# Where the sums of k's exponentials are made in a linear-attention layer: within ScalarE's exponentials or by a VectorE reduction

## The chip, the cores and the metric

The kernel runs on one core of a Trainium2 chip. That core has five engines that work side by side and wait for each other by semaphores: TensorE (PE, matmuls; its weight loads are listed as PEld), VectorE (DVE), ScalarE (ACT), GpSimd (POOL) and SyncE (SP), which here issues the transfers. The metric is the device time of one execution in microseconds (us), and the time given is the median of several executions.

## The reference

An input x of 32 batches x 256 tokens x 256 features goes through four residual layers in a row. Layers 0 and 2 are Mamba layers (a selective scan over time with 512 channels and 16 states), layer 1 is softmax attention with 16 heads, and layer 3 is linear attention. All are modulated by a condition vector. The change lies in layer 3, which is, cut to what matters:

```python
xn = layernorm(x, norm_scale, norm_bias)
q, k, v = xn @ Wq + bq, xn @ Wk + bk, xn @ Wv + bv
k = where(mask, -inf, k);  v = where(mask, 0, v)        # then split into 16 heads
q = softmax(q, axis=-1)                                 # over a head's 16 features
k = softmax(k, axis=2)                                  # over the 256 tokens
attn = einsum('bhse,bhsd->bhed', k, v)
y = einsum('bhtd,bhed->bhte', q, attn)
h = layernorm(y) * (1 + scale) + shift                  # scale, shift from the condition
x = x + silu(h) @ film_out_W + film_out_b
```

The softmax of k runs over tokens. Each of the 256 features of k has its own maximum and its own sum of 256 exponentials.

## The kernel before

All arithmetic is fp32. A batch is worked on whole: 256 tokens x 256 features, as two groups of 128 partitions. A Mamba layer is split into a part ahead of the scan (`mamba_ahead`: norm, input projection, convolution, the steps `dt` and `dtu` that go out to memory and come back spread over the partitions as `dtr` and `dtur`) and the scan itself (`mamba_scan`). The scan has 16 steps, numbered k, each over 128 partitions x 1024 elements. Step k takes these operations:

- POOL makes `b`, the product of `dtur` and `B` (tile `b`, a ring of four buffers).
- ACT makes `h`, four exponentials of `dtr` (a ring of two PSUM buffers).
- DVE runs the recurrence over time, a scan, into `h` on even k and on odd k into `b`.
- The product with `C` is made by DVE on even k and by POOL on odd k (the last step of layer 2 counts as even).
- PE sums over states into `y`, which frees the `b` buffer. After every eighth step DVE multiplies `y` with a gate into `u`.

The scans of the layers 0 and 2 of different batches follow each other without a break: in the steady state a scan of layer 0 for one batch and a scan of layer 2 for the batch two before it take turns. Everything else (the parts ahead of the scans, attention and linear attention) is placed between the scan's steps on the same engines.

The order on every engine is not written by hand. The layers are Python generators that call `at(cost)` and then an engine. `at` opens a `Step` with a planned cost in us and a due time. `Plan.call` records the operation in the step, and `use` records which tiles it reads and writes. `Plan.order` then plays the steps forward with these costs and picks for each engine the step with the earliest due time among those that can begin soon. `carry_out` issues them all in that order, from one line, L468, so that nearly every instruction in the profile has that line. Several constants steer it. `SHIFT` holds one offset for the due time of each step of a layer, the same in every batch. `NEED` says how much work PE must have had lately for the plan to leave it alone. Where there is less, `usual` may put a filler matmul on PE, `y<-rows,zeros`, which adds zero to `y`. `LATE` and `NEAR_ACT` bear on which step ACT takes next when steps need different activation tables. `Exp`, `Silu` and `Softplus` are used with different tables, and a change of table is an instruction of its own on ACT (`ACT_TABLE_LOAD`).

In `linear_attention` k lies with features on partitions and tokens along the row, in PSUM. DVE takes the row maxima (`kmx`), POOL clamps and negates them, ACT makes the exponentials `ke` in two instructions of 128x256 with `kmx` as bias, DVE sums each row into `ks` and takes the reciprocal, and ACT multiplies `ke` by it. Then PE transposes `ke` (`tr_k`), and ACT copies the result to `kvt`, from which PE makes `kv`.

Of the kernel before, what the change touches and what calls it, by code (L numbers as in the profile page):

```python
# [8 lines left out]
F32 = mybir.dt.float32  # L9
I32 = mybir.dt.int32  # L10
AF = mybir.ActivationFunctionType
ALU = mybir.AluOpType
AX = mybir.AxisListType
# [3 lines left out]
P = 128  # L17
S = 256
D = 256
DC = D // P  # L20
# [36 lines left out]
for _n, _k in COLS:  # L57
# [20 lines left out]

SHIFT = {
    "0": (  # L80
        -33, -39, 49, 69, -13, -21, 58, -32, -13, -36, 7, -37, -50, -1, -44, -40, -43, -13, 18, -41, -36, -47,
        -80, -79, 24, -26, -5, -17, -9, 34, 75, -49, 27, 18, 56, 17, 69, 59, 79, 79, 74, 63, -22, 38, -56, -58,
        -50, -76, 3, 14, -1, 41, 23, 28, 53, 49, 6, 61, 34, 75, 75,
    ),
    "0s": (
        -8, -74, -45, -9, -61, -75, -1, 18, -58, 23, 27, -12, -1, -16, 19, 64, -41, -18, -5, 59, 23, 65, -13,
        20, 8, 65, -63, -5, 65, -77, 21, 57, 80, 76, 71, 79, 66, 53, 57, 74, 49, 72, 52, 46, 36, 25, -46, -3,
        -67, 6, 60, 26, -19, 29, 74, 64, 56, 18, 73, 13, 26, 22, 44, 17, -8, 73, 38, 40, 71, 77, 60, 57, 74, 51,
        40, -47, 6, 32, -43, 61, 52, 16, 53, -20, -75, -25, -43, 15, 27, -41, 46, -76, -9, -10, -47, -3, 33,
        -22, 42, -77, -43, -22, -10, -2, -29, 57, 17,  # L90
    ),
    "1": (
        -64, -4, -23, -21, 49, 48, -49, -43, -80, -32, -70, -18, 3, 3, -25, -46, -54, -70, -75, -1, -8, -30, 34,
        79, -14, -67, 8, -5, 14, -36, -52, -14, -7, -22, -60, 9, -59, -18, -64, 1, 1, 26, -16, 17, 46, -30, -15,
        32, 9, 30, -12, 10, -20, 42, -47, -14, 23, -22, -68, 27, 32, 19, 2, -1, -80, -62, -79, -54, -79, -47,
        -25, -15, -21, -10, 1, 21, -2, 31, -58, 2, -3, -49, 6, 78, -43, -6, -35, 11, 23, -14, -58, 40, 44, -1,
        -23, -50, 2, -35, -73, -69, -17, -5, -2, -79, -57, 27,
    ),
    "2": (
        -18, 34, 39, -51, -30, -27, 5, 75, -63, -79, -32, -5, -41, -36, 42, -64, -65, -11, -35, 3, -13, -46,  # L100
        -43, -42, -41, -54, -68, 20, -39, -29, -57, -67, -21, -5, -32, 54, 2, -58, 50, -60, 12, -44, -37, 5, 71,
        7, 64, -66, -80, -44, -71, -78, -63, -69, -78, -80, -79, -53, -5,
    ),
    "2s": (
        27, -39, 3, -15, 79, -10, 35, -22, 71, 45, -25, 54, -1, 32, -7, 37, 53, -22, 60, -60, 9, -12, -10, 6,
        -9, -23, -5, -37, 29, 26, 15, 11, 42, -10, 70, -30, -11, 26, 48, 26, -67, -61, -52, 27, -1, 57, -35,
        -14, -16, -33, 27, 39, 23, -38, 41, -5, 0, -3, 40, -60, 6, -49, -5, 43, 75, 47, 47, 59, 18, 50, 11, 65,
        42, 55, 24, 46, 47, 43, 52, 64, 64, 29, 5, -35, 2, -56, 30, -23, 43, -61, 5, -20, -47, -18, 40, -26,
        -80, -66, -78, 31, -53, 1, -35, -55, 7, 41,
    ),  # L110
    "3": (
        -5, 8, -23, -48, -53, -70, -75, -55, -50, -34, 7, -31, -45, -58, -61, -75, -43, -72, -18, -76, 6, 0,
        -79, -42, -57, 45, 9, 77, 33, -38, -7, -34, 44, -52, 12, 32, -55, -56, -69, 46, -68, -67, -79, -53,
    ),
    "w": (
        73, 75, 58, 71, 33, 47, 28, 57, 27, 50, 16, 34, 52, 42, -58, -10, -11, -12, -6, 9, 47, 25, 58, 59, 17,
        70, 19, 12, -23, 30, -51, -46, -77, -80, -32, -40, -10, 21, 69, 76, 72, 80, 72, 80, 72,
    ),
}

# [130 lines left out]
class Plan:  # L251
# [1 line left out]


    NEAR = 0.36
    NEED = 1.12
    IDLE = 0.47
    LATENCY = 0.15
    SWITCH = 1.3
    LATE = 0.04  # L260
    NEAR_ACT = 0.76

    def __init__(self, nc, tc):
        self.nc, self.tc = nc, tc
# [5 lines left out]
    def at(self, cost, then=0.0, ahead=0.0, area=None):  # L270
        self.kind[1] += 1
        shift = SHIFT.get(self.kind[0], ())
        n = self.kind[1]
        ahead -= 0.01 * shift[n] if n < len(shift) else 0.0
        self.step = Step(cost, self.due - ahead, then, 2140 * cost if area is None else area)
        self.step.kind = tuple(self.kind)
        self.step.number = len(self.steps)
        self.steps.append(self.step)
        return self.step

    def call(self, engine, name, args, kw):
        s = self.step
        assert s.engine in (None, engine)
        s.engine = engine
        s.calls.append((name, args, kw))
        if name == "activation":
            f = args[2]
            table = None if f in (AF.Identity, AF.Copy) else f
            assert s.table in (None, table) or table is None
            s.table = s.table or table  # L290
        out = kw.get("out", args[0] if args else None)
        for a in (*args, *kw.values()):
            if isinstance(a, View):
                self.use(s, a, a is out)

    def use(self, s, view, written):
        t = view.tile
# [15 lines left out]
    def order(self):  # L313
# [41 lines left out]
        def usual(found, t0):  # L355
# [4 lines left out]
            end = at + s.cost  # L360
            if clock.recent(end - clock.STRETCH, end) + s.area >= self.NEED * clock.ENOUGH:
                return one
# [7 lines left out]
        def best(e):  # L370
            found = []
            for s in can[e]:
# [5 lines left out]
                if e == "scalar" and s.table not in (None, table):  # L378
                    more, due = self.SWITCH, due + self.LATE
                found.append((begin + more, due, s.number, s, begin, more))  # L380
# [6 lines left out]
            if e == "scalar":  # L387
                near = self.NEAR_ACT
            return min((f for f in found if f[0] <= t0 + near), key=lambda f: (f[1], f[2]))
# [103 lines left out]
def kernel(ctx: ExitStack, tc: tile.TileContext, t, out: bass.AP):  # L493
    nc = tc.nc
# [174 lines left out]
    for L in (0, 2):  # L669
        Aneg[L] = ctile([P, IC, QB, SG], f"Aneg{L}")  # L670
        a = Aneg[L].rearrange("p c q g -> p (c q g)")
# [28 lines left out]
    nc = plan  # L700
    at = plan.at

    def space(name, bufs, **kw):
        return Space(ctx.enter_context(tc.tile_pool(name=name, bufs=bufs)), bufs, **kw)

    xp, w2, w1 = space("xp", 5), space("w2", 2), space("w1", 1)
    bcp, rep, ring, small = space("bcp", 5), space("rep", 2), space("ring", 4), space("small", 4)
# [110 lines left out]
    def transposed(src, nm):  # L818

        ps = mm(f"tr_{nm}")  # L820
        pv = ps.rearrange("p (c t) -> p c t", c=2)
        at(0.5, area=0.0)
        for c in range(2):
            for s in range(2):
                nc.tensor.transpose(pv[:, c, s * P : (s + 1) * P], src[:, s, c * P : (c + 1) * P], ident)
        return pv
# [213 lines left out]
    def by_token(xn, w, bias, nm):  # L1040

        ps = mm(nm)
        pv = ps.rearrange("p (s d) -> p s d", s=ST)
        for s in range(ST):
            at(0.96)
            for k in range(DC):
                nc.tensor.matmul(pv[:, s, :], lhsT=xn[:, k, s * P : (s + 1) * P], rhs=w[:, k, :],
                                 start=(s == 0 and k == 0), stop=False)
        at(0.9)
        nc.tensor.matmul(ps, lhsT=one_at(bias, P), rhs=row(bias), start=False, stop=True)  # L1050
        return pv
# [112 lines left out]
    def linear_attention(b):  # L1164
        nm = f"3_{b}"
# [6 lines left out]
        pv = ps.rearrange("p (c t) -> p c t", c=DC)  # L1172
# [6 lines left out]
        kmx = small.tile([P, DC], F32, name=f"kmx_{nm}", tag="kmx")  # L1179
# [2 lines left out]
        at(0.25)  # L1182
        nc.gpsimd.tensor_scalar(kmx, kmx, 0.1 * FAR, -1.0, ALU.max, ALU.mult)
        ke = w1.tile([P, DC, S], F32, name=f"ke_{nm}", tag="ke")
        at(0.9)
        for c in range(DC):
            nc.scalar.activation(ke[:, c, :], pv[:, c, :], AF.Exp, bias=kmx[:, c : c + 1])
        ks = small.tile([P, DC], F32, name=f"ks_{nm}", tag="ks")
        at(0.85)
        nc.vector.tensor_reduce(out=ks, in_=ke, axis=AX.X, op=ALU.add)  # L1190
        nc.vector.reciprocal(ks, ks)
        at(0.74)
        for c in range(DC):
# [1 line left out]
        pv = transposed(ke, f"k{nm}")  # L1195
# [6 lines left out]
        pv = by_token(xn, wt["L3_v"], "L3_v_b", f"v_{nm}")  # L1202
# [6 lines left out]
        pv = by_token(xn, wt["L3_q"], "L3_q_b", f"q_{nm}")  # L1209
# [15 lines left out]
        pv = transposed(q, f"q{nm}")  # L1225
# [7 lines left out]
        pv = ps[:, : DC * P].rearrange("p (c e) -> p c e", c=DC)  # L1233
# [9 lines left out]
        pv = ps.rearrange("p (s d) -> p s d", s=ST)  # L1243
# [71 lines left out]
    for begin, L, b in sorted(layers):  # L1315
        begin = max(begin, end)
        end = begin + (LINEAR[1] if L == 3 else max(0.5, min(ATTN, until[b] - begin)))
        ends[L, b] = end
        layer = (attention if L == 1 else linear_attention)(b)
        gens.append((f"{L}", placed(layer, begin, end, (L, b), (L - 1, b))))  # L1320
        if L == 1:
            until[b] = max(until[b], end)
# [105 lines left out]
```

## Time and profile before

| what | value |
|---|---|
| median of 3 executions | 4544.42 us (4538.73 to 4545.05) |
| the profiled execution, its own time | 4539.75 us |
| its span, first to last instruction | 4537.7 us |
| mean granted TensorE clock | 0.977 of full speed |
| busy PE / DVE / ACT / POOL | 4128.3 / 3828.3 / 3515.6 / 3963.5 us |
| matmuls and filler among them, busy | 279.8 us in 990 rows |
| activation table loads | 419 rows, 537.6 us |
| moved by DMA | 583.65 MB, mean 129 GB/s |

A group's row names the line, the engine, the operation and its tiles (written <- read), then the shape and the count; after the bar come the busy time in us, the mean of one in ns, and the idle time of the engine just before these instructions, with what ended that idle time. An fp32 matmul of the program shows as two MATMUL rows. A row of waits gives the total in us, the number of waits and the longest one. A table of stretches gives for each stretch of time the busy time of every engine.

### The profile page before, as it was taken

To read this page: it belongs to the slowest core of one execution; us is meant where nothing else is said; L and a number is where in the kernel's file an instruction comes from. 1 tells how busy PE (TensorE), PEld (TensorE's weight loads), DVE (VectorE), ACT (ScalarE), POOL (GpSimd) and SP (SyncE) were. 2 spreads that over 40 slices of the span, in tenths; PEclk is the share of its full clock that TensorE was granted. 3 is DMA by queue.
4 is the path that set the end of the run, shared out by engine and by line. 5 is a ranking of instruction groups with operands and counts; after the bars stand their busy time and mean duration, and the time that the engine had idled before them with its cause. 6 is when DMAs were issued, how large, how long until landed. Compare 5 with 4: busy or idle time off the path is not lost. (4 is left out here: it accounts for less than half of the span.)

```text
span 4537.7 us, 77776 instructions
## 1 busy us (share of the span) xinstructions
PE 4128.3 (91%) x27576; PEld 2613.8 (58%) x27576; DVE 3828.3 (84%) x3879; ACT 3515.6 (77%) x7373; POOL 3963.5 (87%) x2544
## 2 busy tenths in 40 slices
PE   5889999999999999999999999999999999999987
PEld 4565555556555555565555555555555555556554
DVE  2768889888889898888998888988888988888865
ACT  2657888788887787888788888888778878888764
POOL 1968999889999998999999999999889999989865
PEclk7999999999999999999999999999999999999999
DMA  7433544554444554444554444455444455444322
GB/s 204 117 97 106 140 124 131 144 146 118 132 128 119 144 147 120 129 133 121 146 148 134 125 136 120 127 149 142 122 127 128 119 153 143 133 122 129 103 77 63
DMA packets 309268, 583.65 MB, mean 129 GB/s; under 512 B 45840, under 2 KB 207216, under 8 KB 308880
## 3 DMA queue, kind: packets, MB, share of 16 engines
q1 hardware_dynamic: 308880, 578.69, 46.0%
q8 instruction: 218, 3.57, 0.3%
q14 instruction: 170, 1.39, 0.1%
HBM read 365.19 MB, written 77.73 MB: 98 GB/s over the span
## 5 line engine op out<-in xcount | busy, mean ns | idle before, releaser
L468 POOL TENSOR_TENSOR b<-dtur,B 128x1024 f32<-128x1024 f32 x1024 | 2396.0, 2361 | 202.0 <-PE y L468 163.4
L468 ACT ACTIVATE h<-dtr,Aneg 128x256 f32<-128x256 f32 x4096 | 1700.6, 466 | 339.9 <-DVE b L468 248.1
L468 DVE TENSOR_TENSOR_SCAN h<-h,b 128x1024 f32<-128x1024 f32 x544 | 1240.1, 2284 | 159.8 <-ACT h L468 111.5
L468 POOL TENSOR_TENSOR b<-b,C 128x1024 f32<-128x1024 f32 x480 | 1130.9, 2359 | 116.0 <-DVE b L468 110.1
L468 DVE TENSOR_TENSOR_SCAN b<-h,b 128x1024 f32<-128x1024 f32 x480 | 1094.0, 2279 | 82.0 <-POOL b L468 80.6
L468 PE MATMUL y<-b,sel 128*32 128x256 f32 x8192 | 627.5, 393 | 72.3 <-POOL b L468 39.9
L468 DVE TENSOR_TENSOR b<-h,C 128x1024 f32<-128x1024 f32 x544 | 659.9, 1217 | 11.3
L468 PE MATMUL in<-hT,w_L_in 128*128 128x256 f32 x2048 | 530.2, 401 | 66.4 <-DVE nm L468 46.3
L468 ACT ACT_TABLE_LOAD x419 | 537.6, 1283 | 31.3 <-DMA dtr<-dtd 17.8
L468 PEld LDWEIGHTS in<-hT,w_L_in 128*128 128x128 f32 x2048 | 379.4, 196 | 201.6 <-DVE nm L468 59.7
L468 PEld LDWEIGHTS y<-b,sel 128*32 128x32 f32 x8192 | 185.5, 109 | 374.3 <-issue 124.3
L468 ACT ACTIVATE ex<-s 128x512 f32<-128x512 f32 x512 | 277.2, 594 | 132.8 <-PE s L468 130.1
L468 DVE TENSOR_REDUCE nm<-s 128x2 f32<-128x512 f32 x512 | 327.6, 677 | 52.2 <-PE s L468 52.1
L468 PE MATMUL s<-k,q 32*128 32x256 f32 x2048 | 325.0, 403 | 4.6 <-DVE yg L468 1.6
L468 PE MATMUL s<-q,k 32*128 32x256 f32 x2048 | 295.6, 404 | 8.7 <-DVE nm L468 5.2
L468 PE MATMUL y<-rows,zeros 128*128 128x256 f32 x990 | 279.8, 403 | 0.0
L468 PE MATMUL cv<-xc,taps 128*32 128x256 f32 x2048 | 182.7, 424 | 105.8 <-DMA xc<-xpad 76.2
L468 PEld LDWEIGHTS s<-k,q 32*128 32x128 f32 x2048 | 197.1, 185 | 127.5 <-issue 54.7
L468 PEld LDWEIGHTS s<-q,k 32*128 32x128 f32 x2048 | 178.4, 186 | 126.0 <-issue 49.9
L468 PE MATMUL o<-w_L_out,u 128*128 128x256 f32 x1024 | 243.0, 387 | 8.1 <-DVE u L468 3.9
L468 PEld LDWEIGHTS o<-w_L_out,u 128*128 128x128 f32 x1024 | 189.2, 191 | 56.7 <-DVE u L468 13.1
L468 PEld LDWEIGHTS y<-rows,zeros 128*128 128x128 f32 x990 | 171.9, 192 | 82.5 <-issue 68.2
(480 smaller groups left out, 5581.3 us busy)
## 6 DMA issues: line engine op xcount, KB each, us to landing
dtur<-dtud SPq DMA_DIRECT2D x256, 512.0 KB, 5.3
dtr<-dtd SPq DMA_DIRECT2D x256, 512.0 KB, 6.9
xc<-xpad SPq DMA_DIRECT2D x256, 129.5 KB, 2.4
xc<-xpad SPq DMA_DIRECT2D x256, 129.4 KB, 2.7
xc<-xpad SPq DMA_DIRECT2D x256, 129.2 KB, 2.3
xc<-xpad SPq DMA_DIRECT2D x256, 129.1 KB, 2.4
C<-bc SPq DMA_DIRECT2D x256, 128.0 KB, 2.6
B<-bc SPq DMA_DIRECT2D x256, 128.0 KB, 2.7
```

The costliest lines, as they stand in the source:

```text
L468: made.append(getattr(engine, name)(*[real(a) for a in args], **{k: real(v) for k, v in kw.items()}))
```

## The change

The two exponentials of k get a second output, the row sums (`accum_out`), so that `ks` is written by ACT. The DVE reduction goes, and its reciprocal stays as a step of its own. The planned costs of the two steps change with that (1.1 and 0.15 us in place of 0.9 and 0.85). `Plan.call` now counts `accum_out` as written. The offsets of all steps in `SHIFT`, and the constants `NEED`, `LATE` and `NEAR_ACT`, have other values, so the order of the instructions differs on every engine. Of `SHIFT` only the first row of one entry is shown here; all seven entries are replaced.

```diff
 SHIFT = {
     "0": (
-        -33, -39, 49, 69, -13, -21, 58, -32, -13, -36, 7, -37, -50, -1, -44, -40, -43, -13, 18, -41, -36, -47,
+        -12, -21, 77, 78, 40, 60, 71, -26, -18, -11, -2, -73, -49, -47, -80, -80, -80, -80, -67, -55, -45, -38,
...
     NEAR = 0.36
-    NEED = 1.12
+    NEED = 1.13
     IDLE = 0.47
     LATENCY = 0.15
     SWITCH = 1.3
-    LATE = 0.04
-    NEAR_ACT = 0.76
+    LATE = 0.14
+    NEAR_ACT = 0.52
...
             if isinstance(a, View):
-                self.use(s, a, a is out)
+                self.use(s, a, a is out or a is kw.get("accum_out"))
...
         ke = w1.tile([P, DC, S], F32, name=f"ke_{nm}", tag="ke")
-        at(0.9)
+        ks = small.tile([P, DC], F32, name=f"ks_{nm}", tag="ks")
+        at(1.1)
         for c in range(DC):
-            nc.scalar.activation(ke[:, c, :], pv[:, c, :], AF.Exp, bias=kmx[:, c : c + 1])
-        ks = small.tile([P, DC], F32, name=f"ks_{nm}", tag="ks")
-        at(0.85)
-        nc.vector.tensor_reduce(out=ks, in_=ke, axis=AX.X, op=ALU.add)
+            nc.scalar.activation(ke[:, c, :], pv[:, c, :], AF.Exp, bias=kmx[:, c : c + 1], accum_out=ks[:, c : c + 1])
+        at(0.15)
         nc.vector.reciprocal(ks, ks)
         at(0.74)
         for c in range(DC):
```

## The prediction

> **What bounds the kernel now.** The page first: no engine is at its peak, three are near it.
>
> ```profile
> PE 4128.3 (91%) x27576; PEld 2613.8 (58%) x27576; DVE 3828.3 (84%) x3879; ACT 3515.6 (77%) x7373; POOL 3963.5 (87%) x2544
> ...
> L468 POOL TENSOR_TENSOR b<-dtur,B 128x1024 f32<-128x1024 f32 x1024 | 2396.0, 2361 | 202.0 <-PE y L468 163.4
> ```
>
> Start and end dilute these shares, so I read the busy time of the steady stretch next, then POOL's waits in it.
>
> ```profile
> 400.00:4100.00 3700.00, 3427.36 (x23204) 2154.14 (x23204) 3251.87 (x3261) 3001.89 (x6299) 3387.02 (x2163) 0.99 0.48 132
> ```
>
> ```profile
> POOL b L468 <- PE y L468: 103.2, 89, 2.9
> POOL b L468 <- DVE b L468: 75.5, 77, 3.7
> POOL dtu L468 <- ACT dt L468: 14.0, 25, 0.7
> POOL b L468 <- DMA dtur<-dtud: 10.0, 4, 2.9
> ```
>
> The columns of the stretch are PE, weight loads, DVE, ACT, POOL: 93, 58, 88, 81 and 92%. DVE's row for the permuted residual (x<-x,og) comes at 2115.47 and, seven batches on, at 3051.11 us: 133.7 us a batch. POOL's own work in a batch, from its groups, is 32 x 2.36 (products with B) + 15 x 2.36 (with C) + 2 x 2.35 (dtu) + 1.27 + 4 x 1.34 (norm statistics) + 0.66 = 122.9 us. Its waits between 600 and 4000 us sum to 218 us, over 25.4 batches 8.6 each; 2 us are small gaps. So POOL paces the kernel, and the time follows POOL's waits: for PE's y (a ring buffer comes free) and DVE's scan. The change takes nothing from POOL.
>
> Last the edited operations.
>
> ```profile
> L468 ACT ACT_TABLE_LOAD x419 | 537.6, 1283 | 31.3 <-DMA dtr<-dtd 17.8 <-DVE b L468 3.4 <-PE dt L468 1.6
> ...
> L468 PE MATMUL y<-rows,zeros 128*128 128x256 f32 x990 | 279.8, 403 | 0.0
> ...
> L468 ACT ACTIVATE ke<-ke,ks 128x256 f32<-128x256 f32 x64 | 29.0, 500 | 20.0 <-DVE ks L468 20.0
> ...
> L468 ACT ACTIVATE ke<-k,kmx 128x256 f32<-128x256 f32 x64 | 26.8, 470 | 57.0 <-POOL kmx L468 57.0
> ...
> L468 DVE TENSOR_REDUCE ks<-ke 128x2 f32<-128x512 f32 x32 | 21.2, 662 | 2.4 <-ACT ke L468 2.4
> ...
> L468 DVE RECIPROCAL ks<-ks 128x2 f32<-128x2 f32 x32 | 5.3, 166 | 1.1
> ```
>
> All of the removed work is 21.2 us of DVE, 0.47% of the time.
>
> **The change part by part.** The instruction lists of both builds give counts: DVE 32 fewer, POOL and SP the same (2857 transfers), ACT 53 more, all table loads (421 to 474), PE 237 more, all filler matmuls (495 to 732). The rest is order.
>
> *The reduction goes:* 32 x 0.662 = 21.2 us of DVE. At most all of it returns, if DVE paced everywhere; nothing, where POOL does. DVE idles 12% of the steady stretch, so I credit a third: -7 us.
>
> *The accumulation:* 64 exponentials also write a sum. The trace has no such instruction. Below: 0, or less if it shortened the row, which an added output gives no reason for. Above: one more short ACT instruction each, nearest the shortest ACT row, the copy of xd at 0.36 us: 23 us. I take 0.2 (small DVE and POOL rows of two columns are 0.17 to 0.23): 13 us of ACT. ACT idles 25 us a batch in the steady stretch ((3700 - 3002)/27.7), which hides 0.4; uncovered, it costs those 13.
>
> *A new wait.* Before, v's scaling and an h step stand between exponentials and the multiply by 1/ks, and ACT waits 0.69 us (20.0/29). After, the multiply follows at once. On DVE the reciprocal now stands behind scan 6 (2.28) and its product (1.22). From the end of DVE's kmx: POOL 0.23 and hops, exponentials and sums 1.2, ACT ready at 1.6; reciprocal done at 3.7. ACT waits 2.1, 1.4 more (46 us in all). Behind it stands h 8 (1.67), done 2.6 after the reciprocal; DVE first has x (0.69), scan 7, a reduction and a subtraction, 4.3 us. Cover enough: 0. Transposes of ke follow it on PE; kv, which needs them, is three scan steps from where DVE uses it.
>
> *Table loads:* steady batches go from 13 to 15; dt's second half now stands apart from its first in the L0 scan, with a switch each way. The timeline of ACT shows what a switch costs:
>
> ```profile
> 2243.60 1.67 ACT L468 ACTIVATE h<-dtr,Aneg 128x256 f32<-128x256 f32 x4 [0.48 <-DVE b L468]
> 2245.29 1.28 ACT L468 ACT_TABLE_LOAD   x1
> 2246.59 0.60 ACT L468 ACTIVATE sz<-in 128x512 f32<-128x512 f32 x1
> ```
>
> 0.02 us lie on either side, so 1.30 each: 53 x 1.30 = 69 us of ACT. The Trainium skill (ScalarE: Activation LUTs, section What ACT_TABLE_LOAD costs) speaks harder against the change: 1.28 plus 1.38 of drain, 2.66 us a switch, which makes 141 us. The row decides: no drain is seen. 2.2 us a batch fit in the idle 25; I take 0, and 69 if each stands before an h that DVE awaits.
>
> *Fillers:* one is two rows, 279.8/495 = 0.57 us; 237 make 134 us, 4.2 a batch. PE has 9.8 idle ((3700 - 3427)/27.7). A filler takes the place of idle time or delays a real matmul. Ends: 0 and 134. I take 0, since the steady clock is 0.99 and PE waits for others, and keep 134 as a rival.
>
> *The order, the largest term.* I follow it from the end of the last L2 scan that POOL finishes (step 13), t = 0, in rows: scan 2.28, product 1.22, POOL 2.36. DVE: scan 14, product, to 3.5; scan 15 needs POOL's b 15, now behind C 13, at 4.8, and ends 7.1, its product 8.3. L0's scan 0 ends 10.6; two score reductions, newly first, 12.0; product 13.2, u 13.9, scan 1 16.2. POOL has done b 0 to 3 by 14.2 and waits 2.0 for it. Then its x needs yg (22.1 on DVE): 1.2 more. C 3 needs scan 3, behind two more reductions, 25.8: 2.3 more. So 5.5 in this place; before, the two batches from 2163 us waited 0.73 and 1.91 there. In return POOL's b 0 no longer waits: six long POOL operations now stand between dtu and it (before: four), 4.7 us more for dtu's store and dtur's load, which on SP keep their places behind the store of out; it waited 2.24 and 2.85. The old waits of 2.18 or 0.47 at b 8, 0.55 and 0.63 in L2 go as well, DVE being early there. New: C 13 1.0, C 11 0.9, hops of 0.1 to 0.3 about 1.0; kept: dtu and the memsets 0.9. Sum after 9.3, against 8.6: +0.7 x 28 steady batches = +20 us; with the spread of that walk (2 us a batch) -56 to +60.
>
> The start-up is reordered on SP too (the second x and some weights change places), where POOL waits for first data until 95 us; I take 0, +-5.
>
> *Sum:* -7 + 0 + 0 + 0 + 0 + 20 = +13, and +7 for the wait for the reciprocal and the sums where their cover fails one time in eight ((46 + 13)/8): +20. The profiled execution took 4539.75 us (span 4537.7), 4.7 under the median of 4544.4; against the median that is 4564.
>
> **The rivals.**
> *Faster:* the walk overrates the C 1 and C 3 waits, since DVE's rows overlap, and the end of the b 0, b 8 and L2 waits stays. At 7.7 a batch against 8.6: -25, 4519. At half of those two waits, 6.6 against 8.6: -56, 4488. For: the b 0 wait is 10 us by transfers alone in the view. Against: three reductions and yg now precede scan 3.
> *PE becomes the pacemaker (clearly slower):* fillers do not fill idle time but precede score matmuls. 123.9 + 4.2 busy + 9.8 idle is 137.9 a batch, +4.2 x 28 = +118: 4662. It decides if PE's unfilled idle stays above 5.6 a batch. For: PE is 93% busy. Against: the plan places a filler only where PE's next matmul would start late or leave PE too idle, and most of PE's waits in the steady stretch name DVE or a transfer.
> *Table loads on the path:* +69, 4613. For: DVE waits 71.7 us for h already. Against: ACT's own waits for DVE are 168.9.
> *No change:* reduction and reorder cancel, 4544.
> That the sums stay on DVE is excluded by its list.
>
> **How the numbers follow.** A measurement can tell about 0.2% (9 us). Likeliest: the small loss, 0.36 (4554 to 4600 on its own). Loads or PE on the path 0.13. No change 0.09. The small gain 0.27, the large 0.15. So faster 0.42, same 0.09, slower 0.49. The range leaves out the top of the PE case and the tail of the large gain: 4478 to 4645.
>
> **What would show it.** Right: POOL's waits for DVE b above 3.0 us a batch (now 75.5/25.4), those for PE y below 4; no more than a few us for dtur; ACT's wait for ks near 2 us; loads of 1.28 us. Wrong: a batch below 133.4 us (the gain), PE's idle unchanged beside 732 fillers (PE case), DVE's wait for h well above 71.7 (loads).

## The result, and the profile after

The changed kernel is slower: 4697.5 us (median of 4 executions, 4685.9 to 4708.4) against 4541.7 us. The ratio is 1.0332, with a 95% interval of 1.0313 to 1.0351. The direction was forecast, though by little more than a coin toss (0.49 against 0.42); the size was not: +156 us came where +20 stood, outside the range. The profiled execution has a span of 4684.2 us, at a mean granted clock of 0.975. Nearly all of the loss is there at nearly the same clock: that span is 146 us longer than the one before, which had 0.977. The other three executions, at 0.966 to 0.969, take 11 to 23 us more.

The page after, in its row of engines, and the stretch from 400 to 4100 us (columns as before: PE, weight loads, DVE, ACT, POOL, then PEclk, DMA share, GB/s):

```profile
PE 4234.1 (90%) x28050; PEld 2713.5 (58%) x28050; DVE 3834.8 (82%) x3847; ACT 3591.1 (77%) x7490; POOL 3970.8 (85%) x2544
```

```profile
400.00:4100.00 3700.00, 3397.31 (x22843) 2168.98 (x22844) 3144.79 (x3119) 2965.96 (x6179) 3269.92 (x2083) 0.98 0.46 127
```

POOL does the same 2544 instructions in the same time (3970.8 us against 3963.5), but in the steady stretch it is busy 117 us less (3269.9 against 3387.0): it waits more. DVE's busy time is the same within 7 us, although its reductions are gone; more work is on PE, by its fillers, and on ACT, by its table loads. DVE's rows for `x<-x,og`, taken over 25 batches (from 764.5 to 4133.7 us before, from 789.3 to 4292.0 us after), come 134.8 and 140.1 us apart: +5.3 us a batch. The 133.7 of the prediction is the mean of seven batches and a little low. The loss is spread over the whole steady state. POOL's waits between 600 and 4000 us:

```profile
POOL b L468 <- DVE b L468: 144.5, 92, 2.6
POOL b L468 <- PE y L468: 79.4, 71, 5.7
POOL b L468 <- DMA B<-bc: 71.6, 49, 2.7
POOL x L468 <- DVE yg L468: 22.0, 22, 1.0
```

All rows of that view sum to 329.6 us, over 24.3 batches 13.5 each, where 218 us and 8.6 stood. The wait for DVE has nearly doubled, a row for loads of `B` is new, the rows for `dtur` and for ACT's `dt` are gone, and that for `y` is a little smaller but longest at 5.7 us. The operations of the edit, from the groups:

```profile
L468 ACT ACT_TABLE_LOAD x472 | 605.6, 1283 | 110.1 <-issue 45.6 <-DVE b L468 37.4 <-DMA dtr<-dtd 16.9
L468 PE MATMUL y<-rows,zeros 128*128 128x256 f32 x1464 | 422.4, 411 | 0.0
...
L468 ACT ACTIVATE ke<-k,kmx 128x256 f32<-128x256 f32 x64 | 29.8, 470 | 14.0 <-POOL kmx L468 13.9
L468 ACT ACTIVATE ke<-ke,ks 128x256 f32<-128x256 f32 x64 | 29.0, 501 | 9.7 <-DVE ks L468 9.7
...
L468 ACT ACTIVATION_READ_ACCUMULATOR ke<-k,kmx 128x1 f32 x64 | 12.6, 197 | 0.0
```

The sum is a second instruction of ACT of 0.197 us behind each exponential; the exponential itself keeps its 0.470 us.

Where SyncE stands while POOL waits for `B` is seen in its timeline (start, duration, operation, count), here in one scan of layer 2:

```profile
2290.70 8.87 SPq L468 DMA_DIRECT2D xc<-xpad  x14
...
2302.68 0.59 SPq L468 DMA_DIRECT2D B<-bc  x1
...
2305.88 0.60 SPq L468 DMA_DIRECT2D B<-bc  x1
```

Fourteen transfers take 8.87 us to issue, 0.63 each, and the `B` of steps 2 and 3 stand behind them. POOL, 20 to 60 us earlier in the scan of layer 0, shows other waits:

```profile
2243.62 2.36 POOL L468 TENSOR_TENSOR b<-b,C 128x1024 f32<-128x1024 f32 x1 [2.58 <-DVE b L468]
2248.68 9.28 POOL L468 TENSOR_TENSOR b<-dtur,B 128x1024 f32<-128x1024 f32 x4 [2.71 <-PE y L468]
...
2267.36 2.35 POOL L468 TENSOR_TENSOR b<-dtur,B 128x1024 f32<-128x1024 f32 x1 [5.41 <-PE y L468]
```

The first is C 3, the product with `C` of step 3, which the prediction had at 2.3. The other two are b 5 and b 9, products with `B`, which wait for a buffer of the ring. On PE the sum ahead of b 9 stands behind fillers and attention's scores `s`:

```profile
2261.53 2.08 PE L468 MATMUL y<-rows,zeros 128*128 128x256 f32 x4
2263.53 2.08 PE L468 MATMUL s<-k,q 32*128 32x256 f32 x8
...
2266.16 1.94 PE L468 MATMUL y<-b,sel 128*32 128x256 f32 x16
```

The sum ahead of b 5 stands behind convolutions, `cv`.

### The profile page after: what moved, and what is told of

It reads as the page before. It is cut to its first block, busy times and chain, and to the rows that moved or that the text cites. A ratio compares the mean times of both kernels' runs of the same rounds, so it can differ in the third digit from the quotient of the medians.

```text
span 4684.2 us, 78595 instructions
## 1 busy us (share of the span) xinstructions
PE 4234.1 (90%) x28050; PEld 2713.5 (58%) x28050; DVE 3834.8 (82%) x3847; ACT 3591.1 (77%) x7490; POOL 3970.8 (85%) x2544
## 5 line engine op out<-in xcount | busy, mean ns | idle before, releaser
L468 PE MATMUL y<-b,sel 128*32 128x256 f32 x8192 | 611.8, 395 | 89.3 <-POOL b L468 72.8
L468 PE MATMUL in<-hT,w_L_in 128*128 128x256 f32 x2048 | 540.8, 403 | 33.6 <-DVE nm L468 28.3
L468 PE MATMUL y<-rows,zeros 128*128 128x256 f32 x1464 | 422.4, 411 | 0.0
L468 PE MATMUL s<-q,k 32*128 32x256 f32 x2048 | 333.9, 403 | 7.7 <-DVE nm L468 3.7
L468 PEld LDWEIGHTS y<-rows,zeros 128*128 128x128 f32 x1464 | 258.3, 195 | 137.5 <-issue 115.4
L468 PE MATMUL s<-k,q 32*128 32x256 f32 x2048 | 309.3, 410 | 2.5 <-DVE nm L468 1.1
L468 PEld LDWEIGHTS s<-q,k 32*128 32x128 f32 x2048 | 209.9, 185 | 122.0 <-issue 67.1
L468 PEld LDWEIGHTS o<-w_L_out,u 128*128 128x128 f32 x1024 | 185.0, 190 | 34.8 <-DVE nm L468 11.5
```

Source lines behind the costliest of these rows:

```text
L468: made.append(getattr(engine, name)(*[real(a) for a in args], **{k: real(v) for k, v in kw.items()}))
```

## The experiments

In every experiment the median stands beside the ratio to the kernel before, with its interval, from runs on the same chip. The first question is how much the edit does and how much the order.

**The edit alone, and the order alone.** In the first kernel the plan keeps its old costs, so that every remaining instruction keeps its old place:

```diff
...
         ke = w1.tile([P, DC, S], F32, name=f"ke_{nm}", tag="ke")
+        ks = small.tile([P, DC], F32, name=f"ks_{nm}", tag="ks")
         at(0.9)
         for c in range(DC):
-            nc.scalar.activation(ke[:, c, :], pv[:, c, :], AF.Exp, bias=kmx[:, c : c + 1])
-        ks = small.tile([P, DC], F32, name=f"ks_{nm}", tag="ks")
+            nc.scalar.activation(ke[:, c, :], pv[:, c, :], AF.Exp, bias=kmx[:, c : c + 1], accum_out=ks[:, c : c + 1])
         at(0.85)
-        nc.vector.tensor_reduce(out=ks, in_=ke, axis=AX.X, op=ALU.add)
         nc.vector.reciprocal(ks, ks)
```

> The edit alone: the exponentials of linear attention write their sums through the accumulator, the 32 reductions are gone from VectorE, and every other instruction of every engine stands in the order of the kernel before. Theory (the whole loss is the new order): the edit is worth nothing or a little, 0 to -22 us (-0.5%), with POOL's waits still near 8.6 us a batch. Rival A (the edit itself costs: the read of the accumulator holds ScalarE and what is queued behind it): +50 to +150 us. Rival B (the edit is worth the reductions' share of POOL's waits for VectorE): -1%, -45 us.

4541.8 us, 0.9989 (0.9975 to 1.0002): -5 us, between -11 and +1. The second kernel is the changed one, its costs and shifts untouched, with the reduction put back into the step of the reciprocal.

> The order alone: the changed kernel's order on every engine, with the reduction put back on VectorE ahead of the reciprocal and no accumulator. Theory (the order makes the loss): +3.3%, about 4695 us or a little above, up to +20 us for the reductions. Rival A (the edit makes it): back to 4545 us. POOL's waits would stand at 13 to 14 us a batch by the theory.

4728.3 us, 1.0386 (1.0357 to 1.0415). So the edit is worth 11 us at most, and the whole loss comes with the order. The reduction may be dearer in the new order than in the old: 0.5% by the two ratios, some 25 us, against 5. But this kernel ran at a lower granted clock; at 0.969, in one execution of each, the two kernels of the new order are 14 us apart (4711.8 and 4698.1).

**Is it the tables, or that they are new?** The edit with its two new costs, but the old `SHIFT`, `NEED`, `LATE` and `NEAR_ACT`:

> The edit with its two changed costs, but the planner's shifts and constants of the kernel before: the order is drawn again from the old tables. Theory (the tables belong to one set of costs, and the order is what moves the time): a third order with a time of its own, away from both 4542 and 4697 by more than 1%; its place can't be told from the profile, but one that was fitted to nothing should be worse than the changed kernel's. Rival (the new tables are what is bad): close to 4542.

5012.9 us, 1.1044 (1.1015 to 1.1072). The old tables with costs that differ by 0.2 and 0.7 us in two steps give an order 10% slower. Here the old table of shifts was of no use with costs other than its own; the new one is the better answer to the new costs, and still a worse one than the old order, which the edit could have kept.

**Which engine's order?** The plan was made to replay lists of step numbers, one per engine, so that one engine's list can come from the other kernel:

```diff
+        left = {e: list(reversed(c)) for e, c in CHAINS.items()}
         def best(e):
             found = []
+            if left[e] and left[e][-1] < 0:
+                return (now[e], 0.0, 0, self.idle, now[e], 0.0)
-            for s in can[e]:
+            for s in [s for s in can[e] if left[e] and s.number == left[e][-1]]:
```

Only SyncE's list can be exchanged alone: in every mixture of the two orders on the four computing engines, the engines wait for each other in a circle. Both directions were run.

> The changed kernel with the order of one engine, SyncE's queue of transfers, taken whole from the kernel before; PE, VectorE, ScalarE and GpSimd keep the changed order. Theory (the late B come from SyncE's order, and cost 2 to 3 us a batch): as the hoist of the B alone or better, -40 to -90 us from the changed kernel, 4610 to 4655. Rival (the loss lies in the order of the four computing engines, and SyncE's old order doesn't fit them): within 0.5% of the changed kernel, or slower.

5071.9 us, 1.1164 (1.1139 to 1.1189).

> The mirror of it: the edit alone in the order of the kernel before (4542 us), with only SyncE's queue in the changed order. Theory: the late loads come with the queue, +40 to +90 us, and GpSimd's waits for B appear. Rival (the queue is harmless where the engines keep the old order): within 0.3% of 4542.

4493.7 us, 0.9892 (0.9868 to 0.9917): faster than either kernel. The theory of the first round, that SyncE's new order carries the loss, falls: in the old order of the engines the new queue is a gain of 48 us over the edit alone (4541.8). What it takes away is seen in PE's waits and POOL's. With the edit alone:

```profile
PE cv L468 <- DMA xc<-xpad: 52.5, 18, 4.1
```

```profile
POOL b L468 <- PE y L468: 113.4, 101, 3.1
POOL b L468 <- DVE b L468: 56.3, 50, 3.8
```

POOL's with the new queue:

```profile
POOL b L1420 <- DMA x<-in_x: 41.8, 13, 4.6
POOL b L1420 <- PE y L1420: 26.7, 33, 3.4
POOL b L1420 <- DMA B<-bc: 22.9, 27, 2.1
```

PE's wait for `xc` falls from 52.5 to 1.8 us, POOL's wait for `y` by 87 and its wait for DVE from 56.3 to 0.7. That the sums behind those convolutions come earlier is the likely link, not a shown one. The price is 22.9 us for late `B`, and 59.0 us under the names of two other transfers (`x<-in_x`, and `k<-mterm` with 17.2). All of POOL's waits together go from 229.9 to 153.3 us. The old queue under the new engines does harm instead: POOL's memset of `xpad` waits 166.0 us for the stores of dt (9.5 with the new queue), and the sums are late too:

```profile
POOL b L1428 <- PE y L1428: 280.0, 102, 7.1
POOL xpad L1428 <- DMA dtd<-dt: 166.0, 27, 8.5
```

So the four engines' new order costs 204 us (4697.5 - 4493.7) with the same queue.

**Late loads of `B`.** On SyncE alone, 58 loads stand as early as their buffers allow:

```diff
+    def hoisted(self, order, wanted, after):
+        order = list(order)
+        for s in [s for s in order if wanted(s)]:
+            at = {o: n for n, o in enumerate(order)}
+            last = max((at[o] for o in after(s) if o in at), default=-1)
+            if last + 1 < at[s]:
+                order.remove(s)
+                order.insert(last + 1, s)
+        return order
...
         order = self.order()
+        order = self.hoisted(order, self.early_b, self.frees_b)
```

`early_b` picks the loads of `B` of steps 2 and 3 of layer 2, and `frees_b` gives what frees their buffers.

> The changed kernel with 58 transfers moved forward on SyncE's queue alone: the loads of B of steps 2 and 3 of layer 2's two scans stand among or ahead of the 16 small transfers of xc, not behind them; all other engines in the same order. Theory (GpSimd's 2 to 3 us a batch of waiting for those B are part of the loss): -50 to -80 us, 4620 to 4650. Rival (the wait is hidden behind another that comes next, the sum rings or VectorE): within 0.3% of the changed kernel. A third outcome: the xc transfers that are now later hold layer 2's C5 or VectorE, and it is slower.

4657.4 us, 1.0242 (1.0207 to 1.0278), 40 us less than the changed kernel, a little short of what was expected. POOL's waits in the profiled execution, the slowest of six (4680.5 us at a granted clock of 0.959):

```profile
POOL b L506 <- DVE b L506: 157.5, 103, 2.7
POOL b L506 <- PE y L506: 122.4, 68, 6.1
```

The 71.6 us for `B` are gone to nothing, but the wait for `y` has grown from 79.4 to 122.4 and that for DVE by 13. Not all of this growth need be the edit's: the time of one and the same kernel goes with its granted clock. Here the six executions go from 4629.2 us at 0.971 to 4680.5 at 0.959, and most lie below the changed kernel's 0.966 to 0.975. At 0.966, in one execution of each, the times are 4648.4 and 4708.4: 60 us apart. Why the clock is lower is not shown.

**Late sums.** First, besides the early `B`, sums of layer 0 were put right behind the steps that they follow in the plan (k of neither 0 nor 7 modulo 8), without regard to when their products are there.

> The early B loads as in the run before, and besides the sums of layer 0's scans moved forward in PE's order, each to right behind what it needs, past scores, fillers and products of linear attention. Theory (GpSimd's waits at b 5 and b 9 for a free buffer of the ring are PE's late sums): a further -30 to -60 us, 4600 to 4625. Rival A (the scores behind them are then late, and VectorE and ScalarE wait): no gain, 4650 to 4660. Rival B: the granted clock falls since PE's work is spread otherwise, and it is slower.

4901.6 us, 1.0792 (1.0767 to 1.0816): 244 us lost. PE takes its list in order, so a sum ahead of its product holds everything behind it: its sums wait 126.0 us for products of POOL and DVE, against 42.3 in the changed kernel. Then 640 steps of PE, the sums of both scans and the terms of `u`, were moved, none further than to where the profile of the changed kernel showed its product ready:

> The changed kernel with 640 steps of PE moved forward (sums of both scans and the terms of u), none further than to where the profile of the changed kernel showed its product ready, so that PE doesn't wait for it there. All other queues keep the changed order. Theory (sums that stand behind scores and fillers release GpSimd's ring late: 3 us a batch of waits for y, and part of those for VectorE behind them): -40 to -90 us, 4610 to 4655. Rival (the releases are early, and the wait moves to VectorE's scans): within 0.5% of 4697. The run with sums moved further, ahead of their products, lost 244 us against the one without; by the theory that was PE waiting for the products, which this placing avoids.

4707.5 us, 1.0372 (1.0348 to 1.0397): nothing gained.

```profile
POOL b L1428 <- DVE b L1428: 180.8, 154, 3.4
...
POOL x L1428 <- DVE yg L1428: 51.9, 24, 2.2
...
POOL b L1428 <- PE y L1428: 10.9, 7, 3.9
```

The edit did what it was made for: the wait for `y` is 10.9 us instead of 79.4. The 68 us came back in the rows for DVE (+36 and +30), and the sum of all rows is 335.7 against 329.6. The rival of the expectation was right: DVE is next. With the sums so placed and the `B` early:

> The changed kernel with both mends that did no harm alone: PE's sums where the profile showed their products ready (alone 4707 us) and the 58 loads of B early (alone 4657 us); VectorE's queue stays. Theory (sums, scans and B hand the wait on to each other, so with two of them out of the way only VectorE's is left): a little better than the early B alone, 4600 to 4650. Rival (VectorE's scans take every wait that is removed): 4650 to 4670.

4646.6 us, 1.0232 (1.0207 to 1.0256), not to be told from the early `B` alone.

```profile
POOL b L1454 <- DVE b L1454: 202.3, 157, 3.9
POOL x L1454 <- DVE yg L1454: 51.9, 24, 2.2
```

No row for `B` is left and 2.8 us for `y`, and nearly all of the rest, 254 of 289.7 us, stands in the two rows for DVE.

**DVE's scans.** 592 scans and products moved ahead of attention's reductions and other small operations, to where their inputs were ready:

> The changed kernel with VectorE's queue alone rearranged: 592 scans and products with C moved forward past score reductions, norm statistics and the like, none further than to where the profile of the changed kernel showed its inputs ready. Theory (VectorE's scans stand behind attention's reductions, and GpSimd's 144.5 us of waits for VectorE come from that): -40 to -100 us, 4600 to 4655. Rival (the reductions are then late, PE waits for them in its order and the sums behind them are late too): within 0.5% of 4697 or slower.

5431.4 us, 1.1963 (1.1934 to 1.1991).

```profile
POOL b L1428 <- PE y L1428: 412.5, 85, 10.6
POOL b L1428 <- DVE b L1428: 95.3, 59, 4.0
```

```profile
PE nm L1428 <- DVE nm L1428: 99.8, 27, 4.7
```

POOL's wait for DVE falls from 144.5 to 95.3 us as meant. But the reductions are now late: PE's transposes of their results (`nm`) wait 99.8 us where they waited 29.2, they stand in its list ahead of sums, and POOL waits 412.5 us for those. The clock falls to 0.893, and what share of the loss is the clock's is not told apart. All three mends at once:

> The changed kernel with three queues mended at once: PE's sums and VectorE's scans where the profile showed them ready, and the 58 loads of B early. Theory (each mend alone only passes the wait on to the next of the three): more than the sum of the single ones, 4570 to 4640. Rival (the stages are out of step as a whole, attention ahead of the scan, and no forward move within one queue helps): 4650 or above.

5306.7 us, 1.1704 (1.1677 to 1.1732). The other two mends take off only a part of that. The same move in the version that was the fastest up to then, the early `B` in the old order (below):

> The fastest version so far (the edit, old order of the engines, SyncE's queue of the changed kernel, B early: 4479 us) with VectorE's scans and products moved forward to where its own profile shows them ready (709 steps). Theory (scans first is right on VectorE, since GpSimd waits for them): up to -20 us; GpSimd waits for VectorE only 30 us there. Rival (the old order was balanced, and what is passed is late on PE): +10 to +60.

5193.8 us, 1.1443 (1.1407 to 1.1480). So scans first does harm in the old order as well.

**Table loads.** Half of the channels of layer 2 take `Exp` in place of `Softplus`, without a switch, so that part of `dt` is another number there and only the time counts:

```diff
                 for name, args, kw in s.calls:
+                    if getattr(s, "as_exp", False):
+                        args = [AF.Exp if a == AF.Softplus else a for a in args]
...
+            plan.step.as_exp = L == 2 and c2 == 0
```

> The changed kernel with the softplus of half of layer 2's channels written as a plain exponential (that part of dt is changed), so that 55 table loads fall away and ScalarE's other work and every order stay. Theory (the 53 added loads are only partly hidden: one of them holds layer 2's h5 and costs GpSimd about 1.3 us at C5): -10 to -40 us. Rival A (the loads are the loss: 55 x 1.28 us): -70 us. Rival B (ScalarE has slack enough): within 0.2% of the changed kernel.

4716.7 us, 1.0376 (1.0333 to 1.0419): no gain, with 417 loads in place of 472. Two executions at a clock of 0.970 took 4688 us, against 4698.1 at 0.969 with all loads. So the 55 loads are worth some 10 us at most, and the added ones are hidden, or nearly.

**Fillers.** None of the fillers, the steps without a number, is issued:

```diff
             for s in order:
+                if not hasattr(s, "number"):
+                    continue
```

> The changed kernel with none of its 732 filler products issued (they add zeros to the first sum's bank, so the result is the same), all else in the same order. Rival (PE is the pacemaker, and the fillers' 422 us lie on its path): -118 us or more, that is back to 4580 or below. Theory (GpSimd paces, and waits for late B loads, late sums and late h): -1% at most, unless the clock that the throttle grants falls from 0.975; then slower.

4874.5 us, 1.0724 (1.0695 to 1.0752): 177 us slower than with them. The kernel before without its 495:

> The kernel before without its 495 fillers, all else in the same order. If the fillers hold the granted clock, as the changed kernel's run without them suggests (0.975 to 0.873, +177 us), the clock falls below 0.95 here too and the time rises by 60 us or more. If they are only idle filling: within 0.5% of 4542.

4651.2 us, 1.0242 (1.0213 to 1.0271). The steady stretch, with the clock third from the end, of the changed kernel without fillers and then of the kernel before without them:

```profile
400.00:4100.00 3700.00, 3303.04 (x20836) 2062.09 (x20836) 3011.22 (x2977) 2846.19 (x5909) 3120.90 (x1996) 0.89 0.44 122
```

```profile
400.00:4100.00 3700.00, 3352.66 (x22154) 2077.73 (x22155) 3189.17 (x3192) 2940.18 (x6167) 3315.17 (x2122) 0.94 0.46 129
```

Over the whole run the clock goes from 0.975 to 0.873, and from 0.977 to 0.918. Without 422.4 us of fillers the changed kernel's PE is busy 4267.8 us: the same real matmuls take 456 us more than the 3811.7 that are left of 4234.1. The trace's own clock records hold only 1.0 and 0.5: half clock held for 25.4% of this run, and for 5.1% of the changed kernel's. So the run removes the fillers' work and lowers the clock at once, and can't say what either does alone.

**Faster versions.** The edit in the old order, with SyncE's queue of the changed kernel, and the loads of `B` early:

> The edit in the old order of the four engines with SyncE's queue from the changed kernel (4494 us), and the 58 loads of B moved forward as before. Theory (each late B costs GpSimd its wait, 22.9 us in all in that run's profile): -10 to -25 us, 4470 to 4485. Rival (the waits are taken over): within 0.3%.

4479.0 us, 0.9859 (0.9831 to 0.9886), not told apart from the version without the early `B` (0.9868 to 0.9917). The sums moved forward in the version without the early `B`:

> The same 4494 us kernel, with PE's sums moved forward to where that kernel's own profile shows their products ready (633 steps). Theory (late sums hold GpSimd): at most the 26.7 us that GpSimd waits for y there, 4465 to 4494. Rival (scores and convolutions are late in their place): +10 to +40.

4555.8 us, 1.0041 (1.0023 to 1.0059), 62 us lost: what gained nothing in the new order does harm in the old. Last, with early `B`, the four stores of dtu ahead of those of dt, and dtu's first load right behind them:

> The fastest version so far (4479 us) with SyncE's queue alone rearranged once more: in each scan the four stores of dtu before the four of dt, and the first load of dtu right behind the stores. Theory (GpSimd's first product of a scan waits 2 to 4 us a batch there for dtu's way through memory, 68 us in all under the names of neighbouring transfers): -20 to -60 us, 4420 to 4460. Rival (the load of dt is later by as much, and the scan takes over the wait; or the stores land together anyway): within 0.3% of 4479.

4439.4 us, 0.9776 (0.9749 to 0.9802), the fastest here. POOL's waits ahead of the step and after it:

```profile
POOL b L1446 <- DMA x<-in_x: 39.2, 12, 4.0
```

```profile
POOL b L1420 <- PE y L1420: 82.0, 74, 3.1
```

POOL's waits under the names of loads are gone (39.2 us for `x<-in_x`, 19.9 for `k<-mterm`, 9.2 for `dtur`), and `y`, 31.5 us ahead of the step, has taken over most of them: 137.4 us of waits became 132.9. By step, the wait at b 0 of layer 0 falls from 3.3 to 2.1 us a batch, and smaller ones at b 4 and C 1 rise. The two profiled executions lie only 6 us apart in their spans (4449.0 and 4443.1), since the first was the fastest of its six, while the medians lie 40 apart. At the same granted clock of 0.984 the gain is 16 to 23 us (4450.7 against 4434.7 and 4427.9). So the gain is measured, and its cause is not shown by these profiles.

## Why the prediction was right or wrong

*The bound.* POOL paces and the time follows its waits: right. The waits went from 8.6 to 13.5 us a batch, +4.9, and the period by 5.3.

*The reduction, -7.* Within what was measured for the edit in its own order: -5, between -11 and +1, with the accumulation in it.

*The accumulation, 0.2 each.* Right: 0.197, and 12.6 us in all, hidden.

*The wait for `ks`, 2.1.* Wrong, and harmless: 9.7 us over 29 waits, 0.33 each. ACT waits 13.9 us for `kmx` where it waited 57.0. That it comes later to the exponentials, with the reciprocal nearly done when it gets to the product, is the likely reading.

*Table loads, 0.* Right, and the rival with them on the path (4613) is excluded: 55 fewer loads are worth some 10 us at most. Both prices that were weighed, 1.30 by the row and 2.66 by the Trainium skill (ScalarE: Activation LUTs, What ACT_TABLE_LOAD costs), would have shown on the path as 72 or 146 us. The sign set for this rival misled: DVE's wait for `h` did rise, from 71.7 to 96.1 us, but it was no lower (100.4) with 55 loads fewer.

*Fillers, 0.* No trace shows them as the loss; but "idle filling" was too little. The granted clock falls without them, and either kernel is slower. The Trainium skill (TensorE: Matmul & The Clock Gate, Part 1: The HAM clock gate) has it that the throttled state is the default, that activity releases it, and that the clock is then full or half. The traces agree: 1.0 and 0.5 are all they hold, and without the fillers half clock holds for 25.4% of the time instead of 5.1, and in the old order for 16.5% instead of 4.6. The rival that named PE the pacemaker was near in size (4662), but not by its mechanism. It had the fillers delay score matmuls, and the wait for these did not grow. ACT's, before and after, between 600 and 4000 us:

```profile
ACT ex L468 <- PE s L468: 108.0, 109, 5.6
```

```profile
ACT ex L468 <- PE s L468: 31.2, 77, 1.2
```

DVE's wait for scores went from 26.8 to 20.5, and serving POOL's `y` earlier brought no gain. The sign for this rival was badly chosen too. It asked for unfilled idle of PE above 5.6 us a batch, and 11.5 came ((3700 - 3397.31) / 26.4 batches). A PE that waits for others idles as well.

*The order, +20.* This is the step that failed. The walk follows POOL up to C 3 and from there lets the old waits "go as well, DVE being early there", with little new in their place. POOL's waits by step, added up from its timelines between 600 and 4000 us, in us a batch (foretold is 0 where the walk names no wait):

| where | before | foretold | after |
|---|---|---|---|
| layer 0: b 0 | 2.1 | 0 | 0.3 |
| layer 0: C 1, `x`, C 3 | 1.8 | 5.5 | 5.0 |
| layer 0: b 8 before; b 5 and b 9 after | 1.4 | 0 | 3.0 |
| layer 2: C 3 and C 7 before; C 5 after | 1.2 | 0 | 1.5 |
| layer 2: b 2 and b 3, for loads of `B` | 0 | 0 | 2.9 |
| all else | 2.1 | 3.8 | 0.8 |
| sum | 8.6 | 9.3 | 13.5 |

What the walk named as new up to C 3 was right, and so was the end of the wait at b 0. The waits at b 8 and at layer 2's C 3 and C 7 went as foretold. But three waits that it put at nothing came in other places, 7.4 us a batch: for the ring at b 5 and b 9, for DVE at C 5, and for late loads of `B`. Against them stand 3 us of small waits that it counted and that did not come. The difference of the sums, 4.2 a batch over some 28 batches, is 118 of the 133 us missed. For two of the three the runs show what holds POOL: with the `B` moved forward in SyncE's queue their row is gone, and with the sums moved forward in PE's list the row for `y` falls from 79.4 to 10.9. So two things were left out: SyncE's own time of 0.63 us for each transfer, and the place of each sum in PE's list, behind convolutions, scores and fillers. What holds C 5 is open; with 55 table loads fewer it still waits 1.6 us a batch.

*The signs.* POOL's wait for DVE above 3.0 us a batch (5.9), for PE's `y` below 4 (3.3), none for dtur, loads of 1.28: all came, and with them a loss that they did not tell. The wait for `ks` did not. They were signs of the parts, and none was for a wait that nobody had thought of. The sum of POOL's waits would have been.

*What stays open.* Early `B` gives back 40 of the 204 us by which the four engines' order is slower, or 60 at an equal clock. The rest isn't pinned to a place. Each mend within one engine's list handed the wait to another engine, or made it worse; with `B` and the sums mended nearly all of it stands at DVE. DVE's list can't be exchanged for the old one alone, and moving its scans forward cost 734 us. In the profile of the changed kernel attention stands closer to the scan: its first reduction starts 2.2 us after layer 0's first scan on DVE, against 10.2 before, and from its first reduction to its last output it takes 71 us at the median of 25 batches, against 66. That attention as a whole is out of step is argued from this, not shown; a later attention on all engines at once was not tried.

## What to carry to other kernels

When an edit comes with a new order, run the edit in the old order and the old work in the new order before anything else: here the edit was -0.1%, and the order +3.4%. Where engines hand work to each other through a small ring, a sum of waits says about how much is lost, and not which mend will help: here a step moved ahead of its inputs cost 244 us, and 640 steps moved to just where their inputs were ready gained nothing. When a mend moves the granted clock as well, compare executions at the same clock before you believe the wait rows. And a queue of transfers is an engine like the others: with 0.6 us for each issue, its order was worth 1% in one order of the engines and 8% in the other.

## What the runs showed of the hardware

- ACT's row sum costs a separate instruction of 0.197 us and leaves the 0.470 us of the exponential as they are.
- With fillers of 280 and 422 us on PE the mean granted clock of the profiled executions was 0.977 and 0.975; without them it was 0.918 and 0.873, and the median time 109 and 177 us longer. The trace's clock records are 1.0 or 0.5 and nothing between.
- The time of one kernel goes with its granted clock from execution to execution: with the early `B`, 4629.2 us at 0.971 and 4680.5 at 0.959.
- SyncE issues a transfer of `xc` (129 KB) every 0.63 us, and one of `dtr` (512 KB) holds it no longer (0.54 us at the median). The 16 transfers of `xc` of one scan take about 10 us of its queue (16 x 0.63).
